# Output projection as seven products of halves, layer 0's row maxima taken with layer 1's mask, GpSimd's instructions in source order, and the output norm on ScalarE

## The chip, the cores and the metric

The kernel runs on one core of a Trainium2 chip. A time is what one execution takes on the device, in microseconds. The kernel before takes 3133.63 us, the median of three runs (3131.66 to 3134.02).

## The reference, cut to what matters

Two layers on 32 sequences of 512 nodes with 512 features. Layer 0 is a graph attention with one head, whose scores are a sum of a column and a row; layer 1 is masked attention with 8 heads of 64. After each stand a residual and a layernorm.

```python
# x [32, 512, 512], adj [512, 512] (symmetric, ones on the diagonal)
def layer0(X, A, W, a):                      # W [512, 256]
    h = X @ W
    e = leaky_relu(h @ a[0] + (h @ a[1]).T, 0.2)
    e = e + NEG * (1.0 - A)                  # NEG = -1e9
    out = softmax(e) @ h
    return concatenate([out, h], axis=-1)

def layer1(h, adj, Wq, bq, Wk, bk, Wv, bv, Wo, bo):
    q, k, v = split_heads(h @ Wq.T + bq), ...
    scores = where(adj == 0, -inf, q @ k.T / 8)
    out = softmax(scores) @ v                # heads side by side: 512 columns
    return out @ Wo.T + bo

x = layernorm(x + layer0(x, adj, W, a))
x = layernorm(x + layer1(x, adj, Wq, bq, Wk, bk, Wv, bv, Wo, bo))
```

## The kernel before

Everything is float32; `P` is 128, and a sequence is four blocks of 128 rows. The loop at the end of the listing takes one sequence `b` after another, and in each the eight heads as four pairs, `hp` 0 to 3. One turn over `b` is called a period. A pair's work is: scores of row blocks 0 and 1 (two matmuls and two bank tiles each), then other work that is put between as filler, scores of blocks 2 and 3, `head_blocks`, `head_values` of the pair before, and more filler. The filler belongs to other sequences: layer 0 of `b + 1` and `b + 2`, Q, K and V of `b` and `b + 1`, and the output projection of `b - 1`.

- `head_scores` (L657): TensorE makes scores (L671); VectorE adds the mask and takes each row's maximum in one instruction, `minus_max` (L303); ScalarE takes the exponential and its sum (L680).
- `head_blocks` (L685): eight transposes in 32 by 32 blocks on VectorE (L318), a reciprocal of the sums, their way to DRAM on SP's queue and back, spread over partitions, on GpSimd's queue (`inv`, L694), and sixteen DMAs on SP's queue that finish the transposes (`pt`, L335).
- `head_values` (L700): the products with V (`pav`, L706), and a multiplication by `inv` on VectorE that writes one `ot` tile for each pair (L714).
- `project_two` (L509) and `project_v` (L586) make Q and K, and V, as seven products of halves (Strassen's scheme in Winograd's form) with sums of quarters made ahead (`x1_sums` on GpSimd, L498, its tile is `tx`; the weights' in `weight_sums`, L244 to L249).
- `finish` (L722) is the output projection, one row block of 128 rows at a time: four matmuls of 512 columns, one for each pair's `ot` (L727), an addition into `z`, which is the tile of x1 (L736), and the statistics of the layernorm (L268). A sequence's four calls stand in `hp` 1 and 2 of the next one. `store` (L744) does the norm on VectorE (`ln_norm`, L286) and sends the result out.
- Layer 0: `l0_project` makes h with the two attention columns beside it (`ph`, L255). `l0_columns` sends these columns to DRAM and back as rows that stand in every partition (`rows`, with the four row blocks interleaved, 16 bytes apart). `l0_maxima` (L376) takes the row maximum of the neighbours' column under `mask0`, then `most`, the maximum of a row's scores, by L394 and L395; `l0_write`, `l0_read` and `l0_row` bring `most` to a row in every partition. `l0_scores` (L417) makes the leaky scores transposed in `et`, by ScalarE's Prelu (L430), and adds `mask0t` on GpSimd (L434). `l0_weights` subtracts the row on VectorE (L444) and takes the exponential on ScalarE (L445). `l0_values` (L447) is the product with h (`po`, L452), divided and added to `z`. `l0_add_h` (L361) and `add_bias` (L503) add h and the output's bias on GpSimd. `x1_blocks` (L465) brings the normed x1 into transposed order.

PSUM has eight banks: four for scores (`ps_s`), and four that everything else takes in turn (`ps_m`), so that a tile of the second kind waits for the tile four allocations before it to be read. In SBUF, the tag "p" is a ring of nine tiles (`PB`); "rows", "row", "et", "pt", "t" and "tx" are one tile each; x has three.

What sets the order is the source, for the engines of one set: TensorE, SP, VectorE and ScalarE issue in the order of the text. GpSimd is not in the set, and a planner places its instructions.

```python
in_order = {
    mybir.EngineType.PE, mybir.EngineType.SP, mybir.EngineType.DVE,
    mybir.EngineType.Activation,
}
ctx.enter_context(tc.manual_schedule(engines=in_order))
```

Of the kernel before, what the change touches and what calls it, by code (L numbers as in the profile page):

```python
# [9 lines left out]
F32 = mybir.dt.float32  # L10
# [9 lines left out]
MASK0 = -(2.0**30)  # L20
MASK0_MAX = 5.0 * MASK0
MASKED = -1e30
# [4 lines left out]
def kernel(  # L27
# [17 lines left out]
):  # L45

# [51 lines left out]
        mybir.EngineType.Activation,  # L98
# [11 lines left out]
    mask0 = const.tile([P, NB, N], BF16, name="mask0")  # L110
# [9 lines left out]
    wo_sb = const.tile([P, FC, F], F32, name="wo_sb")  # L120
    bq_sb = const.tile([P, FC], F32, name="bq_sb")
# [69 lines left out]
    def masks0():  # L191
        maskf = first[:, 4 * F :].rearrange("p (c n) -> p c n", c=NB)
        for c in range(NB):
            nc.vector.tensor_scalar(
                maskf[:, c, :], adj_sb[:, c, :], -1.0, -MASK0, ALU.add, ALU.mult
            )

            nc.vector.tensor_scalar(
                mask0[:, c, :].rearrange("p (q i) -> p i q", i=NB),
                maskf[:, c, :].rearrange("p (i q) -> p i q", i=NB),  # L200
                MASK0_MAX / MASK0,
                None,
                ALU.mult,
            )
# [22 lines left out]
    def weight_sums():  # L227
# [6 lines left out]
        for w_t, x_t, view, s in (  # L234
# [15 lines left out]
            yield  # L250

# [124 lines left out]
    def l0_maxima(b):  # L376

        h_sb = st["h", b]
        if b == 0:
            pn = psum("pn")  # L380
            for i in range(NB):
                nc.tensor.transpose(
                    pn.rearrange("p (q i) -> p i q", i=NB)[:, i],
                    h_sb[:, i, 1:2].to_broadcast([P, P]),
                    ident,
                )
        else:
            pn = st["rows", b][:, 1].rearrange("p q i -> p (q i)")
        least = small.tile([P, NB], F32, name=f"least0_{b}", tag="least0", bufs=2)
        for i in range(NB):  # L390
            junk = prob.tile([P, N], F32, name=f"junk_{b}_{i}", tag="p", bufs=PB)
            minus_max(junk, pn, mask0[:, i, :], least[:, i : i + 1])
        most = small.tile([P, NB], F32, name=f"most0_{b}", tag="most0", bufs=2)
        nc.vector.tensor_tensor(most, h_sb[:, :, 0], least, ALU.subtract)  # L394
        nc.vector.scalar_tensor_tensor(most, most, ALPHA, most, ALU.mult, ALU.max)  # L395
        st["most", b] = most

    def l0_write(b):
        d = dram.tile([P, NB], F32, name=f"d_most_{b}", tag="dmost")
        nc.sync.dma_start(d, st["most", b])  # L400
        st["most", b] = d

    def l0_read(b):
        row = prob.tile([P, P, NB], F32, name=f"row_{b}", tag="row", bufs=1)
        nc.sync.dma_start(row, st["most", b].partition_broadcast(P))
        st["row", b] = row

    def l0_row(b):

        row, rows = st["row", b], st["rows", b]  # L410
        to = rows[:, 1].rearrange("p q i -> p (q i)")
        nc.scalar.copy(
            to.rearrange("p (i q) -> p i q", i=NB), row.rearrange("p q i -> p i q")
        )
        st["row", b] = to
# [20 lines left out]
    def l0_row_first():  # L436
        most, row = st["most", 0], psum("pl")
# [3 lines left out]
    def l0_weights(b):  # L441
        et, row = st["et", b], st["row", b]
        for j in range(NB):
# [241 lines left out]
    def head_blocks(b, hp):  # L685
# [5 lines left out]
        nc.sync.dma_start(d.rearrange("j p i -> p j i"), total)  # L691
        inv = act.tile([P, P, NB], F32, name=f"inv_{b}_{hp}", tag="inv")
# [3 lines left out]
        pt = prob.tile([P, 4, 2, FC, NB, G], F32, name=f"pt_{b}_{hp}", tag="pt", bufs=1)  # L696
        move_pair(pt, t)
        st["pt", b, hp] = pt

    def head_values(b, hp, bank=None):  # L700
# [12 lines left out]
        ot = act.tile([P, N], F32, name=f"ot_{b}_{hp}", tag="ot", bufs=6)  # L713
# [6 lines left out]
        st["ot", b, hp] = ot  # L720

    def finish(b, i, chunks=range(FC)):  # L722
# [3 lines left out]
        for c in chunks:  # L726
            nc.tensor.matmul(  # L727
                ps,
                st["ot", b, c][:, i * P : (i + 1) * P],
# [8 lines left out]
        if b == B - 1:  # L738
# [217 lines left out]
```

## Time and profile before

| | |
|---|---|
| median of three runs | 3133.63 us |
| the profiled execution | 3132.73 us |
| its span in the trace | 3131.0 us |
| mean granted TensorE clock | 0.994 |
| instructions | 42011 |
| DMA | 470.75 MB, 150 GB/s on average |
| one period | about 95.2 us |

The span runs from the first to the last instruction in the trace, and the difference to the execution's own time, 1.7 us, lies around it. PE is TensorE (PEld its loading of weights), DVE is VectorE, ACT ScalarE, POOL GpSimd and SP the engine that issues most DMAs. In a list of groups, a row is a source line with its operation, how often it ran, its busy time in all and the mean of one in ns, then the idle time ahead of it on its engine and what ended that. These groups matter for what the change touches:

```profile
L727 PE MATMUL pf<-wo_sb,ot 128*128 128x512 f32 x1024 | 465.1, 602 | 2.2 <-DVE ot L714 2.2
L434 POOL TENSOR_TENSOR et<-et,mask0t 128x512 f32<-128x512 f32 x126 | 144.7, 1164 | 342.7 <-ACT et L430 342.7
L444 DVE TENSOR_TENSOR et<-et,rows 128x512 f32<-128x512 f32 x124 | 77.2, 685 | 0.0
L394 DVE TENSOR_TENSOR most<-h,least 128x4 f32<-128x4 f32 x32 | 28.6, 894 | 1.2
```

In the timelines of the next part, a row is: start in us, time to the last end of the run of like instructions, engine, line, operation, and in square brackets the idle time ahead of it and what ended that.

### The profile page before, as it was taken

The numbers are of one execution on the slowest core, as the hardware profiler recorded it, in microseconds if no ns is written. First come the engines' busy times: TensorE is split into PE (matmuls) and PEld (weight loads), VectorE is DVE, ScalarE is ACT, GpSimd is POOL, SyncE is SP. The second block draws the span as 40 slices with busy tenths as digits, with TensorE's granted clock in tenths as the row PEclk, the third lists the DMA queues.
The fourth block names the chain that finished last, engine by engine and source line by source line (L and its number), as shares of the span: only waits on it lengthen the run. The fifth ranks groups of instructions, "written<-read, shape, count | busy, mean of one in ns | idle before, by whom it ended". The sixth has DMA issues, their size and how long they took to land.

```text
span 3131.0 us, 42011 instructions
## 1 busy us (share of the span) xinstructions
PE 3078.4 (98%) x12612; PEld 1915.9 (61%) x12612; DVE 2485.3 (79%) x5797; ACT 1439.6 (46%) x3089; POOL 805.0 (26%) x901
## 2 busy tenths in 40 slices
PE   7999999999999999999999999999999999999997
PEld 6566666666566666566665666665666666666643
DVE  6778878887888788788878787877888887888775
ACT  3444444444544444444445445445444454444442
POOL 1322232222222222322222322222223223222210
PEclk9999999999999999999999999999999999999999
DMA  5656665556566556655565655566555556555644
GB/s 162 147 137 153 150 171 151 145 138 166 145 160 154 145 150 154 166 153 141 143 164 142 170 152 146 143 160 157 155 146 149 154 147 172 144 151 141 156 118 118
DMA packets 247922, 470.75 MB, mean 150 GB/s; under 512 B 95568, under 2 KB 98128, under 8 KB 247696
## 3 DMA queue, kind: packets, MB, share of 16 engines
q1 hardware_dynamic: 235232, 434.23, 55.0%
q0 software_dynamic: 12464, 33.84, 4.0%
q8 instruction: 101, 1.65, 0.2%
q14 instruction: 125, 1.02, 0.1%
HBM read 132.65 MB, written 34.27 MB: 53 GB/s over the span
## 4 chain that ended last, share of the span: by engine, by line
PE 95%; DVE 2%; SPq 1%; DMA 0%; issue 0%; ACT 0%
PE pw L518 25%; PE ps L671 15%; PE pav L706 15%; PE pf L727 14%; PE pv L594 13%; PE po L452 7%; PE ph L255 7%; SPq L335 1%; DVE t L318 0%; DMA pt<-t 0%; DVE x1t_b L318 0%; DVE p L303 0%; SPq L327 0%; ACT p L680 0%; DMA x1t<-x1t_b 0%
## 5 line engine op out<-in xcount | busy, mean ns | idle before, releaser
L680 ACT ACTIVATE p<-p,least 128x512 f32<-128x512 f32 x1024 | 725.5, 710 | 608.2 <-issue 394.1
L303 DVE CUSTOM_DVE_ANT_0 p<-ps,mask 128x512 f32<-128x512 f32 x1024 | 641.9, 683 | 97.6 <-PE ps L671 97.6
L318 DVE STREAM_TRANSPOSE t<-p 128x512 f32<-128x512 f32 x1024 | 622.0, 674 | 2.1 <-DMA pt<-t 2.1
L671 PE MATMUL ps<-qk 64*128 64x512 f32 x2048 | 512.6, 615 | 3.0 <-DVE least L303 3.0
L706 PE MATMUL pav<-pt,v 128*64 128x512 f32 x2048 | 475.1, 606 | 18.0 <-DMA pt<-t 10.4
L727 PE MATMUL pf<-wo_sb,ot 128*128 128x512 f32 x1024 | 465.1, 602 | 2.2 <-DVE ot L714 2.2
L694 POOL DMA_DIRECT2D inv<-d_tot x256 | 134.0, 527 | 1218.7 <-DMA d_tot<-tot 482.1
L727 PEld LDWEIGHTS pf<-wo_sb,ot 128*128 128x128 f32 x1024 | 186.6, 190 | 275.9 <-issue 247.6
L706 PEld LDWEIGHTS pav<-pt,v 128*64 128x64 f32 x2048 | 139.8, 138 | 338.3 <-issue 258.4
L671 PEld LDWEIGHTS ps<-qk 64*128 64x128 f32 x2048 | 178.2, 186 | 252.1 <-issue 176.7
L255 PE MATMUL ph<-w_sb,xt 128*128 128x258 f32 x1024 | 236.1, 388 | 3.2 <-ACT x1t L483 2.9
L452 PE MATMUL po<-h,et 128*128 128x257 f32 x1024 | 234.2, 387 | 2.1 <-issue 1.9
L434 POOL TENSOR_TENSOR et<-et,mask0t 128x512 f32<-128x512 f32 x126 | 144.7, 1164 | 342.7 <-ACT et L430 342.7
L255 PEld LDWEIGHTS ph<-w_sb,xt 128*128 128x128 f32 x1024 | 194.3, 192 | 54.9 <-issue 22.7
L452 PEld LDWEIGHTS po<-h,et 128*128 128x128 f32 x1024 | 193.9, 192 | 55.0 <-ACT p L680 24.3
L507 POOL TENSOR_TENSOR x<-x,bo_sb 128x512 f32<-128x512 f32 x128 | 158.5, 1273 | 210.4 <-DVE x1t_b L318 191.3
L680 ACT ACTIVATION_READ_ACCUMULATOR p<-p,least 128x1 f32 x1024 | 191.7, 187 | 0.0
L542 ACT COPY p<-pw 128x512 f32<-128x512 f32 x192 | 108.8, 583 | 177.8 <-PE pw L518 175.5
L268 DVE BATCH_NORM_STATS2 stats<-x 128x6 f32<-128x512 f32 x256 | 177.8, 695 | 8.9
L680 ACT ACT_TABLE_LOAD x63 | 80.8, 1283 | 208.6 <-DVE least L303 208.0
L274 ACT ACTIVATE rstd<-mv,eps 128x4 f32<-128x4 f32 (+1 forms) x70 | 20.7, 297 | 324.2 <-DVE mv L269 319.8
L554 DVE SCALAR_TENSOR_TENSOR qk<-pw,bqs_sb,p 128x256 f32<-128x256 f32 x128 | 61.8, 483 | 118.7 <-ACT u L542 78.3
(119 smaller groups left out, 4441.8 us busy)
## 6 DMA issues: line engine op xcount, KB each, us to landing
pt<-t SPq DMA_DIRECT2D x2048, 128.0 KB, 3.4
x<-in_x_dram SPq DMA_DIRECT2D x32, 1024.0 KB, 6.9
inv<-d_tot POOLq DMA_DIRECT2D x256, 128.0 KB, 3.8
xt<-in_xt_dram SPq DMA_DIRECT2D x31, 1024.0 KB, 5.4
x1t<-x1t_b SPq DMA_DIRECT2D x496, 64.0 KB, 2.0
out_dram<-x SPq DMA_DIRECT2D x31, 1024.0 KB, 5.1
rows<-d_att SPq DMA_DIRECT2D x31, 512.0 KB, 3.7
row<-d_most SPq DMA_DIRECT2D x31, 256.0 KB, 5.1
```

The source lines that it names most:

```text
L255: nc.tensor.matmul(ps, lhs(c), rhs(c), start=(c == 0), stop=(c == FC - 1))
L268: nc.vector.bn_stats(stats, z[:, i, :])
L303: nc.vector.tensor_tensor_reduce(out=out, in0=scores, in1=mask, scale=-1.0, scalar=MIN_INIT, op0=ALU.add, op1=ALU.min, accum_out=least,)
L318: nc.vector.transpose(t[:, :, :, i, :].rearrange("p r c q -> p c r q"), src.rearrange("p (c r k) -> p c r k", r=4, k=G),)
L452: nc.tensor.matmul(po, et[:, j, i * P : (i + 1) * P], h_sb[:, j, 2:], start=(j == 0), stop=(j == NB - 1),)
L507: nc.gpsimd.tensor_tensor(z[:, i, :], z[:, i, :], bo_sb, ALU.add)
L518: nc.tensor.matmul(ps[:, k * half : (k + 1) * half], weights(k, c), moving(c), start=start and k == 0 and c == 0, stop=c == FC // 2 - 1, s ...
L594: nc.tensor.matmul(ps[:, k * half : (k + 1) * half], columns(k, c), weights(c), start=start and k == 0 and c == 0, stop=c == FC // 2 - 1, ...
L671: nc.tensor.matmul(ps, qk[rows, 0, i * P : (i + 1) * P], qk[rows, 1, :], start=True, stop=True)
L680: nc.scalar.activation(p, p, AF.Exp, bias=least, scale=-1.0, accum_out=total[:, j, i : i + 1])
L706: nc.tensor.matmul(po[j * D : (j + 1) * D, :], st["v", b, c // 2][:, c % 2, head * D : (head + 1) * D], pt[:, :, j, c, :, :].rearrange("p ...
L727: nc.tensor.matmul(ps, st["ot", b, c][:, i * P : (i + 1) * P], wo_sb[:, c, :], start=(c == 0), stop=(c == FC - 1),)
```

## The change

Five things are edited together.

1. The output projection of a sequence, except the last one, is made by `finish_seven`: seven products of halves, 28 matmuls of 256 columns in all instead of 16 matmuls of 512. The products use quarters of `ot` and of `wo_sb`, sums of `ot`'s quarters (t1 to t4, made on GpSimd, three of them in `ot`'s own place), and sums of `wo_sb`'s quarters (`output_sums`, once). The results are added into `z` by VectorE from PSUM and by GpSimd from copies that ScalarE makes. The function is a generator whose seven steps stand at other places of the loop. `ot` is now two tiles of two pairs each. For the last sequence the weights are put back (`output_weights`) and `finish` is used.
2. Layer 0's maxima use `mask1`, with the neighbours' row brought into the mask's order by a copy on GpSimd; `mask0` lives only in the start. What is sent through DRAM is now `least` instead of `most`; the subtraction that makes `most` happens on the row (`l0_row`, GpSimd), and the leaky form on VectorE (`leaky`, in `l0_weights`). The masked value changes from -2^30 to -2^98 for this.
3. GpSimd joins the engines in source order, and its `inv` DMAs move out of `head_blocks` to a later place (`head_inverse`); `x1_sums` moves from `hp` 1 to `hp` 2.
4. The output's norm is done by ScalarE (`out_norm`), and its statistics are taken in one place (`out_stats`).
5. `store`, `l0_read` and `load_x` stand in `hp` 3 after `head_values`.

The diff, cut:

```diff
-MASK0 = -(2.0**30)
-MASK0_MAX = 5.0 * MASK0
-MASKED = -1e30
+MASK0 = -(2.0**98)
+MASKED = 5.0 * MASK0
...
-        mybir.EngineType.Activation,
+        mybir.EngineType.Activation, mybir.EngineType.Pool,
...
+    def output_quarters():
+        v = wo_sb.rearrange("p c (i d) -> p i c d", i=2)
+        lo, hi = slice(0, FC // 2), slice(FC // 2, FC)
+        return v[:, 0, lo], v[:, 0, hi], v[:, 1, lo], v[:, 1, hi]
+
+    def output_sums():
+        a11, a12, a21, a22 = output_quarters()
+        s1, s2, s4 = (wox_sb[:, i] for i in range(3))
+        nc.gpsimd.tensor_tensor(s1, a21, a22, ALU.add)
+        nc.gpsimd.tensor_tensor(s2, s1, a11, ALU.subtract)
+        nc.gpsimd.tensor_tensor(s4, a12, s2, ALU.subtract)
+        nc.gpsimd.tensor_tensor(a21, a11, a21, ALU.subtract)
+        nc.scalar.activation(a22, a22, AF.Identity, scale=-1.0)
+
+    def output_weights():
+        a11, _, a21, a22 = output_quarters()
+        nc.gpsimd.tensor_tensor(a21, a11, a21, ALU.subtract)
+        nc.scalar.activation(a22, a22, AF.Identity, scale=-1.0)
...
     def l0_maxima(b):
...
-            pn = st["rows", b][:, 1].rearrange("p q i -> p (q i)")
+            pn, mask = prob.tile([P, N], F32, name=f"pn_{b}", tag="p", bufs=PB), mask1
+            nc.gpsimd.tensor_copy(
+                pn.rearrange("p (g i q) -> p g i q", g=4, i=NB),
+                st["rows", b][:, 1].rearrange("p (g q) i -> p g i q", g=4),
+            )
...
-            minus_max(junk, pn, mask0[:, i, :], least[:, i : i + 1])
-        most = small.tile([P, NB], F32, name=f"most0_{b}", tag="most0", bufs=2)
-        nc.vector.tensor_tensor(most, h_sb[:, :, 0], least, ALU.subtract)
-        nc.vector.scalar_tensor_tensor(most, most, ALPHA, most, ALU.mult, ALU.max)
-        st["most", b] = most
+            minus_max(junk, pn, mask[:, i, :], least[:, i : i + 1])
+        st["least", b] = least
+
+    def leaky(t):
+        nc.vector.scalar_tensor_tensor(t, t, ALPHA, t, ALU.mult, ALU.max)
...
     def l0_row(b):
...
-        to = rows[:, 1].rearrange("p q i -> p (q i)")
-        nc.scalar.copy(
-            to.rearrange("p (i q) -> p i q", i=NB), row.rearrange("p q i -> p i q")
+        row = prob.tile([P, N], F32, name=f"row_{b}", tag="p", bufs=PB)
+        nc.gpsimd.tensor_tensor(
+            row.rearrange("p (i g q) -> p i g q", i=NB, g=4),
+            rows[:, 0].rearrange("p (g q) i -> p i g q", g=4),
+            rows[:, 1].rearrange("p (i q) g -> p i g q", i=NB),
+            ALU.subtract,
         )
...
     def l0_weights(b):
         et, row = st["et", b], st["row", b]
+        if b > 0:
+            leaky(row)
         for j in range(NB):
...
+    def finish_seven(b):
+        z = st["x1", b]
...
+        b2, b3 = psum(f"pf2_{b}"), psum(f"pf3_{b}")
+        product(b2, b21, a_(0, 1))
+        product(b3, b22, s_(2))
+        yield
+        add(nc.vector, 0, 0, b2)
+        add(nc.vector, 0, 1, b3)
+        yield
+        to = prob.tile([P, 2, N], F32, name=f"to_{b}", tag="rows", bufs=1)
+        t1, t2, t3, t4 = b12, b22, to[:, :, : 2 * P], b21
+        nc.gpsimd.tensor_tensor(t3, b22, b12, ALU.subtract)
+        nc.gpsimd.tensor_tensor(t1, b12, b11, ALU.subtract)
+        nc.gpsimd.tensor_tensor(t2, b22, t1, ALU.subtract)
+        nc.gpsimd.tensor_tensor(t4, t2, b21, ALU.subtract)
+        yield
+        b1 = psum(f"pf1_{b}")
+        product(b1, b11, a_(0, 0))
+        yield
+        add(nc.vector, 0, 0, b1)
+        yield
+        b4, b5 = psum(f"pf4_{b}"), psum(f"pf5_{b}")
+        product(b1, t2, s_(1), start=False)
+        u2 = copy(b1, "u2")
+        product(b4, t3, a_(1, 0))
+        p7 = copy(b4, "p7")
+        add(nc.gpsimd, 0, 1, u2)
+        add(nc.gpsimd, 1, 0, u2)
+        yield
+        product(b5, t1, s_(0))
+        product(b4, t4, a_(1, 1), start=False)
+        yield
+        add(nc.vector, 1, 1, b5)
+        add(nc.vector, 0, 1, b5)
+        add(nc.gpsimd, 1, 1, u2)
+        add(nc.gpsimd, 1, 1, p7)
+        add(nc.vector, 1, 0, b4)
...
+    def out_stats(b):
+        z, key = st["x1", b], f"1_{b}"
+        for i in range(NB):
+            ln_stats(z, key, i)
+
+    def out_norm(b):
+        z, key = st["x1", b], f"1_{b}"
+        mv, rstd = st["ln", key]
+        ln_inverse(key)
+        shift = small.tile([P, NB], F32, name=f"shift_{b}", tag="shift", bufs=2)
+        nc.vector.scalar_tensor_tensor(
+            shift, mv[:, :, 0], -1.0, rstd, ALU.mult, ALU.mult
+        )
+        for i in range(NB):
+            nc.scalar.activation(
+                z[:, i, :],
+                z[:, i, :],
+                AF.Identity,
+                bias=shift[:, i : i + 1],
+                scale=rstd[:, i : i + 1],
+            )
...
+        seven = finish_seven(b - 1) if b > 0 else None
...
             elif hp == 1:
...
-                    finish(b - 1, 0)
+                    next(seven)
             elif hp == 2:
+                if b > 0:
+                    next(seven)
                 if b > 0 and more:
-                    finish(b - 1, 1)
                     add_bias(b + 1)
             else:
                 if b > 0:
                     if not more:
-                        finish(b - 1, 3)
-                    store(b - 1)
+                        steps(seven)
+                    out_stats(b - 1)
...
+                if b > 0:
+                    ln_root(f"1_{b - 1}")
             head_scores(b, hp, 2)
             head_scores(b, hp, 3)
+            if b > 0 and hp in (1, 2):
+                next(seven)
+            if b > 0 and hp == 3:
+                out_norm(b - 1)
             head_blocks(b, hp)
             if before is not None:
                 head_values(*before)
             if hp == 0:
                 next(values)
+                head_inverse(b, 0)
...
             elif hp == 1:
+                if b > 0:
+                    next(seven)
+                head_inverse(b, 1)
...
                     x1_blocks(b + 1)
-                    x1_sums(b + 1, nc.gpsimd)
             elif hp == 2:
...
-                elif more:
-                    finish(b - 1, 2)
-                    finish(b - 1, 3)
...
+                    next(seven)
+                    if more:
+                        steps(seven)
+                head_inverse(b, 2)
+                if more:
+                    x1_sums(b + 1, nc.gpsimd)
...
+                if b > 0:
+                    store(b - 1)
+                if b + 2 < B:
+                    l0_read(b + 2)
                     load_x(b + 2)
...
+                head_inverse(b, 3)
             before = (b, hp)
+        if not more:
+            output_weights()
```

## The prediction

> **What bounds the kernel now.** I read the busy shares first, then the chain of waits, then the timeline of each engine over one period (one sequence is one period; the median one lasts about 95.2 us).
>
> ```profile
> PE 3078.4 (98%) x12612; PEld 1915.9 (61%) x12612; DVE 2485.3 (79%) x5797; ACT 1439.6 (46%) x3089; POOL 805.0 (26%) x901
> PE pw L518 25%; PE ps L671 15%; PE pav L706 15%; PE pf L727 14%; PE pv L594 13%; PE po L452 7%; PE ph L255 7%; SPq L335 1%; DVE t L318 0%; DMA pt<-t 0%; DVE x1t_b L318 0%; DVE p L303 0%; SPq L327 0%; ACT p L680 0%; DMA x1t<-x1t_b 0%
> ```
>
> TensorE is 98% busy and nearly the whole chain, so time follows TensorE's columns and any new hole between them. TensorE's timeline (start, duration, line; a matmul makes two records):
>
> ```profile
> 1506.48 1.89 PE L594 MATMUL pv<-wv_sb,tx 128*128 128x256 f32 x8
> 1508.21 1.89 PE L594 MATMUL pv<-wvx_sb,tx 128*128 128x256 f32 x8
> ...
> 1515.21 1.99 PE L671 MATMUL ps<-qk 64*128 64x512 f32 x8
> 1517.12 3.70 PE L727 MATMUL pf<-wo_sb,ot 128*128 128x512 f32 x8
> 1520.76 1.99 PE L671 MATMUL ps<-qk 64*128 64x512 f32 x8
> ...
> 1526.26 7.21 PE L452 MATMUL po<-h,et 128*128 128x257 f32 x32
> ...
> 1545.49 1.99 PE L671 MATMUL ps<-qk 64*128 64x512 f32 x8
> 1547.40 3.70 PE L727 MATMUL pf<-wo_sb,ot 128*128 128x512 f32 x8
> 1551.03 1.99 PE L671 MATMUL ps<-qk 64*128 64x512 f32 x8
> 1552.95 3.65 PE L706 MATMUL pav<-pt,v 128*64 128x512 f32 x16
> ```
>
> Each row starts where the last one ends. The same engine in the first sequence, whose third head pair has nothing between its scores:
>
> ```profile
> 113.09 1.99 PE L671 MATMUL ps<-qk 64*128 64x512 f32 x8
> 117.11 2.96 PE L671 MATMUL ps<-qk 64*128 64x512 f32 x8 [2.04 <-DVE least L303]
> 120.00 3.65 PE L706 MATMUL pav<-pt,v 128*64 128x512 f32 x16
> ```
>
> There TensorE waits for VectorE's maxima to free the score banks: 6.91 us from first scores to pav, although the matmuls fill less.
>
> VectorE and GpSimd in the second head pair:
>
> ```profile
> 1516.37 0.69 DVE L303 CUSTOM_DVE_ANT_0 p<-ps,mask 128x512 f32<-128x512 f32 x1 [0.36 <-PE ps L671]
> ...
> 1518.82 2.49 DVE L444 TENSOR_TENSOR et<-et,rows 128x512 f32<-128x512 f32 x4
> ...
> 1530.05 1.02 DVE L714 TENSOR_TENSOR ot<-pav,inv 128x512 f32<-128x512 f32 x1
> ```
> ```profile
> 1512.17 2.27 POOL L434 TENSOR_TENSOR et<-et,mask0t 128x512 f32<-128x512 f32 x2
> 1532.32 1.05 POOL L694 DMA_DIRECT2D inv<-d_tot  x2 [17.89 <-DMA d_tot<-tot]
> ```
>
> GpSimd is idle from 1514.4 to 1532.3, while VectorE does its four subtractions L444. What the two do when both read SBUF:
>
> ```profile
> 45.43 1.13 DVE L249 TENSOR_TENSOR wk_sb<-wk_sb 128x512 f32<-128x512 f32 x1
> ...
> 1584.66 1.76 DVE L394 TENSOR_TENSOR most<-h,least 128x4 f32<-128x4 f32 x1
> ```
> ```profile
> 45.07 1.99 POOL L361 TENSOR_TENSOR x<-x,h 128x256 f32<-128x256 f32 x2 [6.55 <-ACT h L355]
> ...
> 1585.12 1.27 POOL L570 TENSOR_TENSOR p<-p,p 128x512 f32<-128x512 f32 x1
> ```
>
> L249 takes 0.68 alone, here 1.13; its two GpSimd neighbours take 1.99 for a usual 1.30 (2.60 for four at 1505.34). L394, 128x4 numbers, takes 0.16 in its shortest run and ends here with GpSimd's op. A VectorE op with two SBUF inputs and a GpSimd op take turns. Ops with one input in PSUM do not suffer: the maxima at 1548.8 keep 0.61 spacing under GpSimd's L507.
>
> **The change, part by part.** Let S be the start of the second head pair's scores (1515.21).
>
> TensorE columns. A 512-column matmul costs 0.429 x 2 = 0.858 (L727: 3.63 for four, 0.2 of it at the ends); one of 256 costs 1.73 / 4 = 0.432 (L594). Sixteen of the first, 13.72, become 28 of the second, 12.09: -1.63 a period, ends unchanged, for 31 periods. By place: second pair +0.02 (eight for four), third pair's middle -1.70 (four small for four large), third pair's end +0.05.
>
> Third pair's middle. Scores to pav takes 7.46 now (1545.49 to 1552.95). TensorE alone would need 5.76, but VectorE first does x1's transposes and then starts its maxima 3.3 us after the scores, at b=0 (116.39) as at 1548.79. So the floor is the 6.91 of the first sequence: -0.55, not -1.70.
>
> Second pair. GpSimd's new source order puts, after the last mask addition, `l0_row`, `l0_add_h` and the four sums t3, t1, t2, t4 (the built order of its instructions shows this). The last mask addition needs ScalarE's last Prelu (ends 1512.99), so it ends at S-1.0. `l0_row` is a strided add no GpSimd row shows: 1.23 as a contiguous one (L497's spacing), 2.5 if stride doubles it as on ScalarE (L430 1241 against L445 615 ns). I take 1.83, from VectorE's pair with the same 16-byte step (L714 1020 against L736 686 ns). `l0_add_h` takes 2.6: to S+3.4. t3 runs S+3.4 to 4.7. VectorE ends its maxima at S+3.61 and wants `leaky` and four subtractions, each 0.61 with two SBUF inputs: alone they end at S+6.65. Taking turns: leaky to S+5.3, t1 to 6.5, subtraction to 7.1, t2 to 8.4, subtraction 9.0, t4 10.2, two subtractions to S+11.4. VectorE then has four maxima (2.45), two additions (1.25), eight transposes (4.8), the reciprocal and L714 (1.1): ot at S+21.0. Without the turns it would be S+16.2.
>
> Who waits: each po tile takes the bank used four allocations before; the fourth takes pav's, freed by L714. TensorE would reach it at S+16.45 (1526.26 plus three times 1.8), today 0.6 after L714's end. It starts at S+21.1: +4.7 (+4.1 with `l0_row` at 1.23, +5.3 at 2.5). The projections behind it slide along; the next pair starts from TensorE's end, so the hole is not won back.
>
> VectorE's other edits: four norms (0.48 each) and most's two small ops go, two additions come; out_stats lies in the 5.5 us idle during ph. The reciprocal and shift ahead of the fourth pair's transposes cost 0.36, and so delay the 16 pt DMAs; TensorE reaches pav after them with little to spare (1596.68 has 0.38 idle): +0.2 (0 to 0.4).
>
> ScalarE: the four output norms, 0.52 each (L232's spacing), and two copies stand where it idles 8 us; `l0_row`'s 1.12 leaves. Uncovered, they delay the p1 copy, due 5 us later. No new table switch is taken; two of 1.28 would still fit.
>
> GpSimd elsewhere: four z additions at 1.27, the pn copy (0.6 to 2.5) and x1_sums moved later end about 8 us before pw needs tx; if that cover went, TensorE would wait their excess. inv's DMAs queue behind but are used a pair later. A maxima-with-p7 collision stays, now 1.3 against the 0.7 mean excess of L394; the 2.0 of L394 and L395 removed pays for it.
>
> SP: the store now stands behind pt's sixteen issues (10.5) and d_least, and load_x waits for its landing (5.1). x lands near S-4, used at S+0.8: nothing; 4 us later it would start to move GpSimd's sums.
>
> Ends: in the start l0_row_first waits behind two additions, +0.3. In the tail the weights are restored by GpSimd after inv's DMAs (3099.5 now) plus 1.3; the last projection starts at 3100.9, not 3094.25, and its 10.5 us end 2.0 after 3109.50, where pav now starts: +2.0. The last period has no subtractions: -1.6.
>
> Sum: 30 periods x (4.7 + 0.02 - 0.55 + 0.05 + 0.2 = 4.4) = 132, plus 0.7. The profiled execution took 3132.7 (span 3131.0, 1.7 around it), 0.9 below the median of 3133.6: **3265**. With +4.1 and +5.3: 3247 to 3283.
>
> [...]
>
> **Rivals.** (1) VectorE's train lets GpSimd in only once. For it: no row shows five VectorE ops against four of GpSimd. Against: the turns at 45 us. Subtractions end at S+8.95, 2.3 late, hole 2.0: 30 x (2.0 - 0.28) = 52, about 3184. (2) Faster: the sums miss the subtractions, or don't block them. It decides below a delay of 0.6 us, where the hole closes (0.3 spare) and the -0.28 is left. For it: L444 never shows a collision today. Against: GpSimd's queue cannot reach t3 before S+2.8, nor t2 before the product at S+5.5. Time 3132.7 - 8.4 + 0.7 = 3125; with the maxima's wait gone too, 30 x (-1.43): 3090. (3) Longer: GpSimd's strided copies slow enough to hold the maxima and hp0's scores, 1 us more a period: 3295.
>
> **Numbers.** Forecast 0.62, (1) 0.15, (2) 0.18, (3) 0.05. The forecast alone spans 3245 to 3285; with (1), 3150 to 3290 holds about 8 in 10. What a measurement here can tell from no change is 0.2%, 6.3 us. Slower 0.78, same 0.06, faster 0.16, the two last from (2).
>
> **What would show it.** The subtractions' mean near 1.5 us instead of 0.685 and t1, t2, t4 near 1.9; TensorE idle before po, some 4 us thirty times, ended by L714's successor; the third pair's second scores waiting for maxima; 28 output matmuls at 0.432. Wrong if the subtractions stay at 0.69, or po follows pav unbroken.

## The result and the profile after

The changed kernel takes 3296.0 us (median of five runs, 3289.36 to 3299.0), the kernel before 3132.9 beside it: 1.0519 times as long, with a 95% interval of 1.0503 to 1.0534. That is 163 us more; forecast were 132 us more, in a range that ended at 3290. The profiled execution has a span of 3293.9 us. First the busy shares of the changed kernel, then its chain of waits:

```profile
PE 3104.8 (94%) x13356; PEld 2086.7 (63%) x13356; DVE 2629.6 (80%) x5735; ACT 1544.1 (47%) x3246; POOL 1257.9 (38%) x1216
PE 71%; DVE 19%; issue 4%; DMA 1%; SPq 1%; ACT 1%; POOL 0%; DVEq 0%; POOLq 0%; ACTq 0%
```

TensorE's columns are fewer, yet it is "busy" for 26 us more, and 19% of the chain is now VectorE's. TensorE's timeline in one second pair (its scores began at 1692.41), and the scores of the third pair behind it:

```profile
1703.48 1.13 PE L480 MATMUL po<-h,et 128*128 128x257 f32 x4
1704.81 1.30 PE L480 MATMUL po<-h,et 128*128 128x257 f32 x4 [0.20 <-ACT et L473]
1707.89 3.71 PE L480 MATMUL po<-h,et 128*128 128x257 f32 x16 [1.77 <-DVE x L793]
1714.17 2.00 PE L480 MATMUL po<-h,et 128*128 128x257 f32 x8 [2.57 <-DVE ot L750]
1716.01 1.03 PE L546 MATMUL pw<-x1t,wq_sb 128*128 128x256 f32 x4
...
1728.19 1.99 PE L699 MATMUL ps<-qk 64*128 64x512 f32 x8
1730.11 1.99 PE L770 MATMUL pf<-wo_sb,ot 128*128 128x256 f32 x8
1732.21 2.96 PE L699 MATMUL ps<-qk 64*128 64x512 f32 x8
1735.10 3.65 PE L738 MATMUL pav<-pt,v 128*64 128x512 f32 x16
```

From po to pw it takes 12.53 us here and 7.05 in the kernel before. TensorE waits in two places, not one: the second po tile waits for VectorE's additions into z (L793), which read a bank, and the last one for the multiplication that frees pav's bank (L750). The third pair's scores reach pav in 6.91 us, the floor that was forecast. VectorE and then GpSimd in the same pair:

```profile
1696.02 3.03 DVE L415 SCALAR_TENSOR_TENSOR row<-row 128x512 f32<-128x512 f32 x1
1699.09 5.61 DVE L472 TENSOR_TENSOR et<-et,row 128x512 f32<-128x512 f32 x4
...
1713.11 1.00 DVE L750 TENSOR_TENSOR ot<-pav,inv 128x512 f32<-128x512 f32 x1
```
```profile
1692.60 2.14 POOL L432 TENSOR_TENSOR row<-rows 128x512 f32<-128x512 f32 x1
1694.68 2.60 POOL L380 TENSOR_TENSOR x<-x,h 128x256 f32<-128x256 f32 x4
1697.24 1.25 POOL L807 TENSOR_TENSOR to<-ot,ot 128x512 f32<-128x512 f32 x1
1698.57 1.60 POOL L808 TENSOR_TENSOR ot<-ot 128x512 f32<-128x512 f32 x1
1700.25 1.60 POOL L809 TENSOR_TENSOR ot<-ot,ot 128x512 f32<-128x512 f32 x1
```

`leaky` takes 3.03 us here instead of some 0.69 (2.27 on average over 30 periods; GpSimd's row, L432, is late in this one): it waits until GpSimd has done the last additions of h and t3, and gets in where GpSimd leaves a gap. Then the two take turns, one for one, and the four subtractions take 5.61 us instead of 2.49.

Where the 163 us are, by the starts of TensorE's stages in both profiled executions (spans 3131.0 and 3293.9):

| place | more, us |
|---|---|
| start, to the first sequence's second scores | 3.2 |
| first sequence | 6.5 |
| 30 periods between (2860.8 to 3012.2) | 151.4 |
| last sequence and end | 1.8 |

and in one of these periods, as a mean over 29 of them (the last one has less in it):

| stage | before | after |
|---|---|---|
| second pair, po | 7.05 | 12.03 |
| second pair, pw | 12.18 | 12.42 |
| third pair, filler and second scores | 5.55 | 5.00 |
| first pair, second scores to pav | 1.95 | 2.14 |
| everything else | 68.6 | 68.7 |

Of the 5.0 us that po takes more, 4.7 lie ahead of its fourth tile, which in 29 of 30 periods starts 0.05 to 0.06 us after the multiplication (L750) ends, and 0.3 in that tile.

### The profile page after: what moved, and what is told of

Same layout as the page of the kernel before. It is cut to its first block, busy times and chain, and to the rows that moved or that the text cites. A ratio compares the mean times of both kernels' runs of the same rounds, so it can differ in the third digit from the quotient of the medians.

```text
span 3293.9 us, 44765 instructions
## 1 busy us (share of the span) xinstructions
PE 3104.8 (94%) x13356; PEld 2086.7 (63%) x13356; DVE 2629.6 (80%) x5735; ACT 1544.1 (47%) x3246; POOL 1257.9 (38%) x1216
## 3 DMA queue, kind: packets, MB, share of 16 engines
q8 instruction: 108, 1.77, 0.3%
## 4 chain that ended last, share of the span: by engine, by line
PE 71%; DVE 19%; issue 4%; DMA 1%; SPq 1%; ACT 1%; POOL 0%; DVEq 0%; POOLq 0%; ACTq 0%
PE pw L546 23%; PE pv L622 11%; PE pav L738 10%; PE ps L699 10%; PE ph L274 7%; PE pf L770 7%; DVE p L322 4%; DVE t L337 4%; DVE et L472 3%; PE po L480 3%; DVE x1t_b L337 2%; DVE row L415 2%; SPq L354 1%; DVE x L793 1%; DVE ot L750 1%
## 5 line engine op out<-in xcount | busy, mean ns | idle before, releaser
L699 PE MATMUL ps<-qk 64*128 64x512 f32 x2048 | 541.9, 620 | 5.7 <-DVE least L322 2.2
L480 PE MATMUL po<-h,et 128*128 128x257 f32 x1024 | 272.1, 416 | 121.9 <-DVE ot L750 66.4
L699 PEld LDWEIGHTS ps<-qk 64*128 64x128 f32 x2048 | 193.1, 186 | 230.6 <-issue 161.9
L598 POOL TENSOR_TENSOR p<-p,p 128x512 f32<-128x512 f32 x64 | 88.8, 1387 | 323.7 <-ACT p L570 323.6
L793 POOL TENSOR_TENSOR x<-x,u_o 128x512 f32<-128x512 f32 x93 | 117.1, 1272 | 245.4 <-ACT u_o L788 214.1
L770 PE MATMUL pf<-wo_sb,ot 128*128 128x256 f32 x744 | 182.2, 388 | 0.0
L770 PE MATMUL pf<-wox_sb,ot 128*128 128x256 f32 x744 | 179.1, 383 | 0.0
```

The source lines that it names most:

```text
L480: nc.tensor.matmul(po, et[:, j, i * P : (i + 1) * P], h_sb[:, j, 2:], start=(j == 0), stop=(j == NB - 1),)
L699: nc.tensor.matmul(ps, qk[rows, 0, i * P : (i + 1) * P], qk[rows, 1, :], start=True, stop=True)
L770: nc.tensor.matmul(ps[:, k * half : (k + 1) * half], columns[:, c, k * P : (k + 1) * P], weights(c), start=start and k == 0 and c == 0, st ...
```

## The experiments

All medians are of four to six runs of the kernel beside runs of the kernel before on the same chip (medians 3128.8 to 3131.3). "S" is the start of a second pair's scores.

### The four sums at a later place

```diff
             elif hp == 1:
-                if b > 0:
-                    next(seven)
                 head_inverse(b, 1)
+                if b > 0:
+                    next(seven)
```

> Of the changed kernel only the four sums of ot's quarters move: GpSimd makes them after the second pair's inv DMAs instead of ahead of them, when VectorE is done with its subtractions. Theory A (the sums and the subtractions take turns, and that makes the hole ahead of the last po tile): the subtractions L472 fall from 1.47 to about 0.69 us; leaky still waits for the end of l0_add_h, 4.9 us after the pair's first scores, so the subtractions end at about 7.9 instead of 12.2, the multiplication that frees pav's bank at 17.6 instead of 21.6, and the hole is some 1.2 instead of 5.2 us: 30 x 4.0 = 120 us less, 3175 us. Rival B (the hole comes from the row being late: mask addition, strided subtraction and l0_add_h ahead of leaky): leaky ends at 5.5 instead of 6.6, 1.1 us earlier, 30 x 1.1 = 33 us less, 3262 us, with a hole of about 4 us left.

Measured: 3144.4 us, 1.0043 (1.0028 to 1.0057) of the kernel before, 149 to 152 us less than the changed kernel. VectorE in the second pair (S is 1524.45):

```profile
1528.06 0.69 DVE L415 SCALAR_TENSOR_TENSOR row<-row 128x512 f32<-128x512 f32 x1
1528.78 2.50 DVE L472 TENSOR_TENSOR et<-et,row 128x512 f32<-128x512 f32 x4
```

Theory A holds, and by more than it said. The subtractions are back at 0.71 us and po takes 7.35. In this period GpSimd's inv DMAs also stand at S-4.9, in the one shown above at S-3.1, so that add_h ends when `leaky` wants to start. That is mostly the choice of the two periods: over 30 of them add_h ends at S+4.0 instead of S+4.4 on average, `leaky` takes 0.82 us instead of 2.27, and the subtractions end at S+7.0 instead of S+11.7. Theory A had read the late period as the rule, and so let `leaky` wait. Rival B falls: with the strided subtraction at 2.14 us as before, the earlier row is worth some 0.4 of these 4.6 us, and nearly nothing of the hole is left. The collision of sums and subtractions is the cause of nearly all of the loss.

### GpSimd's order alone

```diff
-                head_inverse(b, 0)
                 if more:
                     l0_scores(b + 1, [2, 3])
                     l0_row(b + 1)
+                head_inverse(b, 0)
```

> Of the changed kernel only the first pair's inv DMAs move, from ahead of GpSimd's last two mask additions to behind l0_row. Theory A: the mask additions no longer wait behind the inv DMAs, which wait for the sums' way through DRAM; l0_row starts about 1.2 us earlier, and with it add_h, the sums and the subtractions, so the hole shrinks by 0.9 to 1.2 us: 27 to 36 us less, about 3265 us. Rival C (the row's start does not matter, since GpSimd and VectorE end their nine operations together only as late as VectorE's maxima let them begin): no change, 3296 us.

Measured: 3313.2 us, 17 more than the changed kernel, which neither theory said. The row does start earlier (at S-1.0 in every period, instead of S-0.4 on average), but the two inv issues of 1.05 us now stand between it and add_h, so that `leaky` ends at S+6.5 instead of S+5.9 on average, and the fourth po tile starts 0.45 us later, 14 us in 30 periods. The clock behind it differs too. TensorE's timeline at one last po tile (its eight records took 2.00 us in the changed kernel above and take 3.49 here), and the windows of the same time, with the length, the busy time of the five engines and then the granted clock:

```profile
1625.92 3.49 PE L480 MATMUL po<-h,et 128*128 128x257 f32 x8 [2.56 <-DVE ot L750]
```
```profile
1623.00:1626.00 3.00, 0.44 (x3) 0.08 (x1) 2.96 (x8) 0.00 (x0) 0.00 (x0) 0.93 0.02 1
1626.00:1629.30 3.30, 3.30 (x9) 2.67 (x10) 2.95 (x9) 0.00 (x0) 1.05 (x2) 0.55 0.72 163
1629.30:1632.00 2.70, 2.70 (x14) 2.39 (x13) 2.42 (x6) 0.00 (x0) 0.00 (x0) 1.00 1.02 256
```

After 2.56 us of waiting the granted clock is 0.55 for 3.3 us, and a matmul starts every 0.43 us instead of every 0.215. Such stretches come in 27 of the 30 periods here, in 14 in the changed kernel. Where one meets the last po tile or pw, nothing hides it: that is 22 us in the 30 periods here, 13 in the changed kernel. Where one meets the tiles before, behind the wait of 1.77 us for L793, it costs nothing, since the last tile waits for the multiplication anyway, and only waits 0.9 us instead of 2.57. Shorter waits ahead of pav give some 5 us back.

### GpSimd left to the planner

```diff
-        mybir.EngineType.Activation, mybir.EngineType.Pool,
+        mybir.EngineType.Activation,
```

> The changed kernel with GpSimd left to the planner, as in the kernel before; nothing else differs. The built order then has most of l0_add_h, l0_row and the mask additions in another sequence, and the four sums directly behind the mask additions. Theory A: t3 and t1 end before VectorE's maxima do, but t2 must wait until the products have read its place (5.6 us after the pair's first scores) and so t2 and t4 meet the last two subtractions: these end at 8 to 9.5 instead of 12.2, the hole is 1.2 to 2.5 us, about 3190 us (3170 to 3215). Rival J (source order alone makes the hole): 3145 us or less. Rival K (the order makes no difference as long as sums and subtractions are in the same stretch): 3290 us.

Measured: 3263.6 us, between theory A and rival K, nearer to K. The planner also puts the sums where VectorE subtracts: L472 has a mean of 1.42 us, the sums 1.58 to 1.60 each, po takes 11.52 us. t2 waited only 0.3 us a period for the products; the turns had made it late enough by then. So source order is not the cause by itself, the place of the sums is. The first sequence, on the other hand, takes 88.9 us instead of 94.2 with the planner's order.

### Useless work in the hole

```diff
-        for j in range(NB):
+        for j in [*range(NB)] * (2 if b > 1 and i in (0, 2) else 1):
             nc.tensor.matmul(
                 po,
```

> The changed kernel, with the eight matmuls (records) of the first and of the third po tile made twice from sequence 2 on; the second time writes the same sums again, so TensorE does 2 x 4 matmuls of 257 columns (some 3.4 us) a period of useless work in the time in which it waits for VectorE. Theory L (after a wait of 2 us and more the granted clock is halved for some 2.5 to 3.5 us, and that adds to the hole): the waits become shorter or vanish, the last po tile and the projections behind it run at full clock in every period, L480's slow records go from 18 of 30 periods to few, and the time falls by 10 to 25 us in spite of the additional work: about 3278 us. Rival M (the slow stretches do not come from the wait, but from the collision or from chance): the same number of slow periods, 3296 us or more, up to +100 if the useless work is not covered.

Measured: 3270.1 us, 26 less than the changed kernel, with 480 more matmul records. TensorE's waits, in the changed kernel and in this one (us in total, times, longest):

```profile
PE po L480 <- DVE ot L750: 66.4, 29, 2.6
PE po L480 <- DVE x L793: 44.0, 30, 1.8
```
```profile
PE po L480 <- DVE ot L750: 19.5, 30, 0.8
```

VectorE is nearly as late as before (the multiplication ends at S+20.7 instead of S+21.1 on average), TensorE repeats products instead of waiting, no po tile of the 30 periods runs at the halved clock, and the 30 periods take 2984.3 instead of 3012.2 us: 27.9 less. Some 13 us of this are the last po tile (1.84 instead of 2.05 us) and pw (12.18 instead of 12.42) at full clock, as much as the spacing of the records gives for the changed kernel, where 14 periods have slow records, not the 18 of the expectation, and 8 of them in these two places. Some 9 us are the earlier multiplication and 5 are shorter waits ahead of pav; why these changed is not shown. Theory L holds, for about half of the 28 us: a hole costs its length, and a stretch at half clock behind it where nothing hides that.

### The third pair's maxima: four tries

```diff
             elif hp == 2:
+                if more:
+                    x1_blocks(b + 1)
                 if b > 0:
                     next(seven)
```

> Of the changed kernel only x1's four transposes on VectorE move, from ahead of the third pair's first maxima to behind the first four of them. Theory A (the third pair's second scores wait for maxima that stand behind these transposes): from the pair's first scores to pav it takes 5.76 instead of 6.91 us, 30 x 1.15 = 34 us less, about 3262 us. Rival D (the wait goes to the next place, the second four maxima, the transposes of the pair, or the x1 DMAs that now start 2.5 us later): the 1.15 us come back within the period, 3296 us or more.

Measured: 3373.4 us, 77 more than the changed kernel. The third pair's scores reach pav in 5.76 us, as theory A had it; rival D has the rest. TensorE's wait at the fourth pair's pav:

```profile
PE pav L738 <- DMA d_att<-att: 69.5, 23, 8.2
```

The name is that of the DMA that ended last; what TensorE needs is the third pair's pt, and in SP's queue sixteen x1 issues (some 0.65 us each, 10.4 in all) stand ahead of pt's sixteen. Starting them 2.5 us later makes pt late, and the next pair's scores to pav take 4.87 instead of 2.07 us.

> The three moves of the last three runs together: sums behind the second pair's inv DMAs, first pair's inv DMAs behind l0_row, x1's transposes behind the third pair's first maxima. Theory A: no sum meets a subtraction, the row is there when VectorE's maxima end, and the scores of the third pair do not wait. Against the kernel before a period then has -1.70 (third pair), +0.06 (ends of matmul runs), +0.2 (pav of the first pair) and at most +0.3 (hole): 30 x -1.1 = -34, and the start and first sequence +8, the end +2: about 3110 us, faster than the kernel before. Rival E (GpSimd's sums block VectorE wherever they stand, now in the norms and statistics behind po): a new hole of 1 us or more in the second pair's projections, 3140 us or more.

Measured: 3251.6 us. The hole in po is nearly gone here too (7.67 us), and the same wait for pt costs 2.9 us in the fourth pair's scores and 1.5 in its pav on average. Theory A falls for this combination, but rival E's place is wrong: the new hole is not where the sums are. The next try puts the transposes earlier (shown without its other moves):

```diff
-                steps(two)
-                if more:
-                    x1_blocks(b + 1)
+                blocks = x1_blocks(b + 1) if more else iter(())
+                next(two)
+                for _ in two:
+                    next(blocks, None)
+                steps(blocks)
```

> The sums behind the second pair's inv DMAs, as in the run with only that; x1's four transposes one by one between the four results of the projection ahead (VectorE is idle there for some 0.9 us each time), so that they are done before the third pair's scores and SP's queue gets its x1 DMAs earlier, not later; the first sequence's inv DMAs behind l0_row; the last sequence's weights put back ahead of its inv DMAs. Theory A: against the run with the sums alone (3144 us) the third pair's scores to pav fall from 6.91 to 5.76 us, 30 x 1.15 = 34 us; the first sequence gains 2 to 5, the end 3 to 5: about 3103 us, faster than the kernel before by some 27. Rival G (SP's queue or the results of the projection become the bound, as when the transposes were moved back): 3144 us or more.

Measured: 3242.8 us, 1.0363 (1.0346 to 1.0380): 98 us more than with the sums alone. VectorE's wait, then TensorE's first scores of a third pair:

```profile
DVE x1t_b L337 <- PE pw L547: 91.1, 31, 4.2
```
```profile
1597.96 1.99 PE L700 MATMUL ps<-qk 64*128 64x512 f32 x8 [2.94 <-DVE qk L583]
```

The transposes write a tile that shares its place in SBUF with tx (both have the tag "tx", one buffer), so the first of them waits until the projection's products have read tx, and the projection's results stand behind it on VectorE. Neither theory had thought of this; the edit moved a wait onto the path.

The two runs from this kernel are read against it, not against the others:

```diff
     def out_norm(b):
...
-        shift = small.tile([P, NB], F32, name=f"shift_{b}", tag="shift", bufs=2)
...
+        for i in range(NB):
+            ln_norm(z, key, i)
```

> The last kernel with the output norm on VectorE again (four subtract-and-multiply instructions of 0.48 us in the same place, the shift left out). Theory A: the norms stand ahead of the fourth pair's transposes, which set pt's DMAs and so the first pair's pav: 4 x 0.48 - 0.16 = 1.8 us later, of which some 0.2 us were spare, so 30 x 1.6 = 48 us more, about 3150 us. Rival H (that pav is not set by these transposes): no change, 3103 us.

Measured: 3278.1 us, 35 more. The size is near to theory A's, the place is not: the first pair's scores to pav grow by 0.1 us alone, but the four norms make the multiplication behind the transposes late, and the fourth pair's pw, which needs its bank, takes 13.1 instead of 12.3 us; the second pair's po takes 0.6 more. At this place the norm belongs on ScalarE.

```diff
     def finish_seven(b):
...
+        p0 = rows(0)
+        yield
+        add(0, p0)
+        yield
+        yield
+        p1 = rows(1)
+        yield
+        add(1, p1)
+        yield
+        p2 = rows(2)
+        yield
+        p3 = rows(3)
+        yield
+        add(2, p2)
+        add(3, p3)
```

> The kernel with the four moves, but with the output projection of the kernel before (16 matmuls of 512 columns in four row blocks, added into z by VectorE; no sums, no copies), at the same places of the loop; all other parts of the change stay. Theory A: the seven products are worth their columns, 1.63 us a period, as long as nothing waits for their sums: 30 x 1.63 = 49 us more, about 3152 us, that is some 20 us above the kernel before, because what the other parts cost at the start and in l0_row stays. Rival I (their extra work on GpSimd, ScalarE and VectorE costs as much as the columns save): within 10 us of the kernel with the four moves.

Measured: 3269.7 us, 27 more. In the 30 periods of the profiled executions it is 44 us, 1.46 a period, nearly all in the third pair's middle (3.94 instead of 2.34 us); some 7 us come back in the start and in the first and last sequences, and the rest is the distance of the profiled runs from their medians. In these periods the seven products are worth most of their columns (1.46 of 1.63 us), where their sums collide with nothing; of the whole time it is 27 of the 49 us expected.

### The first and last sequence, and a kernel that is faster

```diff
             elif hp == 1:
-                if b == 0:
-                    l0_output(1)
-                else:
-                    if more:
-                        l0_weights(b + 1)
-                        l0_add_h(b + 1)
+                if more:
+                    l0_weights(b + 1)
+                    l0_add_h(b + 1)
+                if b > 0:
                     next(seven)
...
                 steps(values)
-                if b == 0:
-                    l0_weights(1)
-                    l0_add_h(1)
...
-                if b > 0 and more:
+                if more:
                     l0_output(b + 1)
...
+                else:
+                    output_weights()
                 head_inverse(b, 3)
             before = (b, hp)
-        if not more:
-            output_weights()
```

> The kernel with only the sums moved behind the second pair's inv DMAs, and two edits outside the steady periods: in the first sequence layer 0's subtractions and products for sequence 1 stand where they stand in every later sequence (VectorE is not held by l0_row ahead of the pair's maxima), and in the last one the weights are put back ahead of the fourth pair's inv DMAs. Theory A: the first period falls from 95.7 to about 91 us, the end by 3 to 5 us: 3144 - 8 = 3136 us. Rival N (the first sequence is late by the start's DMAs, the end by the clock, not by these orders): 3144 us.

Measured: 3145.8 us, no gain as a whole. The first sequence falls from 95.7 to 91.7 us and the end by 3.3, as theory A had it, but the steady periods are 0.26 us longer each than in the run with the sums alone, where nothing was edited. What does that is not settled; single periods of one run differ by more (94.7 to 96.7 us).

The last two kernels add, to this one, first the transposes two by two (the first `next` does two, the second two and ten DMAs on SP's queue, `steps` the other six on ScalarE's), then a split of pt:

```diff
             head_scores(b, hp, 0)
+            if hp == 2 and more:
+                blocks = x1_blocks(b + 1)
+                next(blocks)
             head_scores(b, hp, 1)
+            if hp == 2 and more:
+                next(blocks)
...
             head_scores(b, hp, 3)
+            if hp == 2 and more:
+                steps(blocks)
```

> The kernel of the last run, with x1's four transposes two by two between the third pair's first maxima (VectorE: two maxima, two transposes, two maxima, two transposes), and 6 of the 16 x1 DMAs on ScalarE's queue behind that pair's exponentials, so that SP issues 10 of them, 6.3 instead of 10.1 us, before pt's sixteen. Theory A (the third pair's wait is the maxima behind the transposes, and moving them cost more than it gained only because SP then issued pt's DMAs 2.5 us late): scores to pav falls to about 5.8 us with no new wait at the fourth pair's pav: 30 x 1.1 = 33 us below the kernel of the last run, about 3103 us, faster than the kernel before. Rival O (the six DMAs on ScalarE delay its copies or x1's arrival, and a wait of the same size stands elsewhere): 3130 us or more.

Measured: 3139.3 us, 6.5 less than the kernel without it, not 33. Rival O's size, but a cause of its own: the third pair gains 0.9 us, and 0.8 of it goes at the fourth pair's pav, for the pt DMAs on SP's queue.

```diff
+        if hp == 2:
+            move_pair(pt, t, some=slice(0, 10))
+            st["rest", b] = pt, t
...
                     if more:
                         steps(seven)
+                move_pair(*st["rest", b], nc.scalar, slice(10, 16))
                 head_inverse(b, 2)
```

> The kernel with x1's transposes two by two (3139 us), and the third pair's last 6 of 16 pt DMAs also on ScalarE's queue, behind its two copies for the output projection, so that SP issues 10 of them, 6.3 instead of 10.1 us. Theory P (the 1.1 us that the third pair gives up are taken back at the fourth pair's pav, which waits for the pt DMAs of the third pair on SP's queue: scores to pav there 2.84 instead of 1.92 us on average, and 0.2 more in the third pair's last products): these waits go, a period falls from 95.2 to about 94.1 us, 30 x 1.1 = 33 us, 3106 us, faster than the kernel before by 0.7%. Rival Q (the six DMAs wait behind ScalarE's copies, or the copies behind them, and the products or pav wait as long): 3130 us or more.

Measured: 3116.2 us, 0.9956 (0.9943 to 0.9970) of the kernel before: 15 us faster than that, and 23 faster than the kernel of the last run. The fourth pair's scores to pav are at 1.92 us, the 30 periods take 2836.2 instead of 2860.8 us, 0.82 less each; theory P's place is right and its 33 us are 23. The first sequence and the start still take 5.6 us more than before, the end 2.4.

## Why the prediction was right in mechanism and wrong in size

- **The collision.** Right, and shown by the move of the sums. L472 is at 1.469 us (said: near 1.5), t1, t2 and t4 at 1.58 to 1.59 (near 1.9; a sum only waits out the rest of one subtraction). Rival 1, GpSimd gets in only once, falls: it gets in between every two subtractions. Rival 2 falls, and rival 3 has the time (3295) but not its cause: the strided copies hold nothing in the fourth pair.
- **The hole.** 4.7 us were forecast ahead of the fourth po tile, bounds 4.1 to 5.3, and 4.7 were measured: the tile starts at S+21.1, as said. That it fits so closely is in part luck, for the parts behind it were off in both directions. "The last mask addition ... ends at S-1.0": on average the row behind it starts at S-0.4 (at S+0.2 in the period shown), since the inv DMAs of the first pair stand ahead of it in GpSimd's new order and wait for the sums' way through DRAM. `l0_row` takes 2.13 us, between the bounds of 1.23 and 2.5, not the 1.83 taken, and `leaky` ends at S+5.9, not S+5.3. The turns behind that are shorter than said, 1.7 us instead of 1.9, and so the subtractions end at S+11.7 where S+11.4 was said. TensorE's waiting is in two pieces: the additions of b2 and b3 free a bank of the ring as well, and the prediction followed only pav's. The first piece costs nothing more, since the fourth tile waits for pav's bank in any case. (The list of waits has 3.7 us a period as idle, since a matmul's modelled end counts as busy and slow records fill part of the waits.)
- **The step that failed** is "the next pair starts from TensorE's end, so the hole is not won back", which stopped one term short: it prices a hole at its length, and what comes behind it was put at nothing. The last po tile takes 2.05 us instead of 1.74 and pw 12.42 instead of 12.18 on average, 0.55 us a period and 16 us in all. Of these, 13 are the half clock, by the records and by the run that filled the hole; the other 3 are there at full clock too (1.84 us for a tile that starts behind a wait). Of the 30 us that were missing, 16 are here and 11 in the ends, below. The profile of before showed the half clock, in a row of its first sequence:

```profile
142.22 5.35 PE L706 MATMUL pav<-pt,v 128*64 128x512 f32 x16 [3.93 <-DMA d_att<-att]
```

  Sixteen records that take 3.65 us in the steady periods took 5.35 after 3.93 us without work, and the granted clock was 0.50 from 143.36 us on, for 3.41 us. In the changed kernel's clock records it is halved 22 times: 14 times for 3.41 us, six times for 6.83, once for 10.24 (in the start) and from 3286.69 us to the end. In its periods TensorE was not idle as long as 3.93 us before: the half clock came behind waits of 2.57 us, and in 6 of the 14 periods already behind the one of 1.77 us.
- **The ends.** Said: +0.3 in the start and nothing in the first sequence. Measured: 3.2 and 6.5. In the start the two mask additions ahead of `most` take 2.66 us, since they meet GpSimd's additions, and the adjacency matrix landed 1.8 us later; but kernels of the experiments with the same start are at its end after 72.9 to 76.2 us (75.2 in the changed kernel, 72.0 before), so a part of the 3.2 belongs to this one execution. The first sequence does layer 0's subtractions for sequence 1 ahead of the second pair's maxima, and the prediction took every period to be alike. VectorE waits there 4.1 us for the row behind the inv DMAs, the mask additions and the strided subtraction, the subtractions meet add_h, and TensorE waits, again with slow matmuls behind it (9.75 us instead of 7.68):

```profile
97.28 9.75 PE L480 MATMUL po<-h,et 128*128 128x257 f32 x32 [6.05 <-ACT et L473]
```

  The last sequence and the end were said to cost 0.4 and cost 1.8.
- **Right as they stood:** the third pair's floor (-0.55 said and measured) and the columns (+0.07 said, +0.06 measured). The first pair's pav (+0.2 said, +0.19 measured: 2.14 us instead of 1.95) is right as a number only. In the runs with the sums late and with the inv DMAs late the same two instructions stand ahead of the transposes, and it is at 2.01 and 2.00; the cause that was forecast is not shown.
- **In one sum:** 30 x 4.4 + 0.7 = 133 were said; 30 x (4.7 ahead of the fourth tile + 0.3 in it + 0.24 in pw - 0.55 + 0.06 + 0.19 + 0.08 in other waits ahead of pav) = 151, and 11.5 at the ends, make 162 of the 163 measured.

## What to carry to other kernels

Before work is put on an engine that has time, look at which instructions of its neighbour it will run beside, and not only at its own idle time: four sums of 1.3 us on an idle GpSimd cost 5 us a period in one place and almost nothing 15 us later. A hole on TensorE is priced with the half-clock stretch that can follow it; here the profile of before had one such row to read it from (5.35 us instead of 3.65). A number read from one period is checked against the mean of all: the period shown above was a late one, and it misled two expectations. A saving on the busiest engine is worth only what the next queue in line, here SP's 32 DMA issues in a row, leaves of it.

## What the runs showed of the hardware

- `leaky`, coming while GpSimd's instructions ran back to back, waited through them in 27 of the 30 periods of the changed kernel, up to the 0.08 us that GpSimd left ahead of t1, and took 1.82 to 3.67 us; in the period shown it waited 2.3 us, through the rest of two additions and t3. Not so in the other three: twice it took 0.69 us, and t3 took 1.81 instead of 1.25 to 1.28, and in the period at 1196.86 us, as in the first sequence, it took 1.17 and 1.15, and VectorE's subtractions took turns with additions of h that ran back to back (1.09 to 1.21 and 1.12 to 1.25 us each; alone 0.68 and 0.64). What decides is not settled.
- A VectorE instruction with one SBUF tensor and two scalars per row (the norm, 0.54 us alone) takes 1.49 to 1.50 in half of the cases in which it meets one of GpSimd's additions (22 of 44 in the changed kernel); transposes, statistics and maxima from PSUM beside such additions keep their times (0.68, 0.67 and 0.69 us).
- The changed kernel became 26 us faster (3270.1 instead of 3296.0) when TensorE was given useless matmuls in place of waits of 1.8 and 2.6 us.
- Whether a wait of 2.57 us is followed by the half clock changes from period to period: 27 of 30 periods have slow records in the kernel with the inv DMAs late, 14 in the changed kernel with nearly the same waits. In the clock records the half clock goes with how little TensorE was busy. The halved stretches of one execution start within 0.003 us of one grid of 3.41 us steps (7 stretches in the kernel before, 22 in the changed one), and over 29 periods of each of those two kernels a step in which TensorE was busy for at most 1.36 us was followed by the half clock every time (21 steps, 7 of them in the changed kernel), one with more than 1.76 us never; between, both happened. With the useless matmuls no step had less than 2.58 us, and none was halved.
